# Start of a graph-network layer: which queue issues the filter taps, x and the first filter stores

## The chip, the cores and the metric

The kernel runs on one core of a Trainium2 chip. A core has a matrix engine (TensorE, PE in the profile, with its weight loads shown as PEld), a vector engine (VectorE, DVE), a scalar engine (ScalarE, ACT), GpSimd (POOL) and SyncE (SP), each with an instruction queue of its own, and 16 DMA engines that move data between HBM and the on-chip memory. SP, ACT and POOL issue transfers. The time is device microseconds of one execution; the figure for a kernel is the median of its runs.

## The reference, cut to what matters

Inputs are `x` (64 graphs, 256 nodes, 256 channels) and `adj` (64, 256, 256).

```
h  = relu(layernorm(x))
c  = relu(bn1(conv1x1(h)))
c  = bn2(conv17(c, w2, pad=8))                 # 17 taps, 256x256 channels
x_conv = relu(c + h)
s  = h @ w_se.T + b_se
A  = exp(-|s_i - s_j|^2) * adj
x_nmp = A @ relu(h @ w_msg.T + b_msg)
out = x + GRU(input=[x_conv, x_nmp], state=h)
```

## The kernel before

Graphs are handled in pairs; pair `i` is one tile `x` of 128 x 1024 elements, loaded by two transfers of 256 KB (`load_x`, `load_rows`, L377). Four pairs make a block, and eight blocks are run. The 17-tap convolution is done in a transformed domain: the sequence is cut into 16 phases, a hand-written transform (class `Fft`, on DVE) turns the activations into 16 frequency points, matrix products with transformed filters are made per point (`products`), and the transform is undone. The transformed filters are made once, at the start, and kept in HBM.

That start is what the change touches. The raw filter is read as `taps`: 128 input channels of each half `dc` in 19 groups of seven channels, so that a group fills 7 x 17 = 119 partitions. `load_taps(dc, a, b, eng)` (L451) loads groups a to b of one half in one transfer. A third has six groups, 119 x 6 rows of 1 KB, 714 KB. The nineteenth group is left over and comes by `load_last_taps` (L456), 34 KB for each half. `points` (L569) are three constant matrices with the roots for three sets of frequency points, called passes 0, 1 and 2.

`filters(m, g, eng)` makes group g for pass m: four matmuls in the trace, two for each half (L479), into an `acc` bank; one copy by ACT into `fo` (L646), of which there are six buffers; and one store of `fo` to the HBM tensors `filt` by the queue `eng` (L647). A copy into `fo` must wait until the store that used the same buffer six calls ago has landed. There are 57 such calls. The list `steps` begins with all three passes of groups 0 to 5, which need the first third of the taps alone, and goes on pass by pass with the other groups.

The first 16 calls are made among the work on the first block, in the loop over j from 0 to 3 (L877). A round j does: `transpose_h(j)` for j > 0 (PE transposes the normed x, ACT writes `hT` with a relu, L599, and at its end `load_x(j + 2)` is issued into the buffer that was just read), `norm(j + 1)` for j = 1 and 2 (DVE statistics L517 to L522, GpSimd's power L523 into `rstd`, DVE's scaling L526), `conv1(j)` (PE, then ACT into `h1`, L618), the first steps of the transform (DVE, L62 and L65) and four calls of `filters`. Round 0's `transpose_h(0)` and `norm(1)` stand ahead of the loop. In round 2 a set of small loads is issued too: nine on GpSimd (L890, L893, L467) and `w_msg` and the first `adj` on SP.

After the loop the other 41 calls of `filters` run, with stores on SP and GpSimd in turn, while DVE does the transform. When the stores of a pass have landed, `load_kind` (L658) reads the transformed filters back as `wb`. All later blocks follow.

The order on each engine is the order in which the code is written (`manual_schedule`). [...] In the kernel before SP issues, in this order: x0, x1; half 0, first third; x2; half 0, second third; four stores; x3; the last third of both halves and the two small loads; four stores; x4, `w_msg`, `adj`; four stores; x5; four stores; and then its share of the later stores. ACT issues half 1's first third, the points and half 1's second third.

## Time and profile before

| | |
|---|---|
| median of 5 runs | 1898.44 us (1896.26 to 1901.28) |
| profiled execution: time | 1899.55 us |
| profiled execution: span | 1897.8 us |
| PE busy in the span | 1836.1 us (97%) |
| DVE busy | 1398.1 us (74%) |
| ACT busy | 637.5 us (34%) |
| POOL busy | 206.4 us (11%) |
| mean granted TensorE clock | 0.989 |

Times in the profile are microseconds from the start of the span. A line of a timeline has the start, the length, the engine, the source line, the operation, output and inputs, and in square brackets the time that the engine was idle before it and what ended that wait. An SP or ACT line with a q is an issue of a transfer: it occupies the queue and not an arithmetic engine, and its length is how long the queue was held in it. Lines for the same group are merged (x4), and a merged length runs from the first start to the last end. A table by stretches of time gives busy microseconds of each engine, the clock granted to TensorE as a share of full speed, the mean busy share of the 16 DMA engines, and the rate.

### The profile page before, as it was taken

To read this page: it belongs to the slowest core of one execution; us is meant where nothing else is said; L and a number is where in the kernel's file an instruction comes from. 1 tells how busy PE (TensorE), PEld (TensorE's weight loads), DVE (VectorE), ACT (ScalarE), POOL (GpSimd) and SP (SyncE) were. 2 spreads that over 40 slices of the span, in tenths; PEclk is the share of its full clock that TensorE was granted. 3 is DMA by queue.
4 is the path that set the end of the run, shared out by engine and by line. 5 is a ranking of instruction groups with operands and counts; after the bars stand their busy time and mean duration, and the time that the engine had idled before them with its cause. 6 is when DMAs were issued, how large, how long until landed. Compare 5 with 4: busy or idle time off the path is not lost.

```text
span 1897.8 us, 21985 instructions
## 1 busy us (share of the span) xinstructions
PE 1836.1 (97%) x7710; PEld 1140.2 (60%) x7710; DVE 1398.1 (74%) x2675; ACT 637.5 (34%) x1335; POOL 206.4 (11%) x324
## 2 busy tenths in 40 slices
PE   6899999999999999999999999999999999999997
PEld 3677445875549554694458755495546944586543
DVE  5777648996499945998389964999559983798522
ACT  2424322243313443244222433134432352324311
POOL 2110110100111010111101001101101111010000
PEclk9889999999999999999999999999999999999999
DMA  5776331662328431482316613174314813063010
GB/s 177 251 245 198 93 80 35 193 178 56 85 49 243 108 93 52 115 235 56 89 34 194 178 55 84 52 239 111 89 55 111 240 56 78 23 190 99 1 44 22
DMA packets 179071, 217.63 MB, mean 115 GB/s; under 512 B 85038, under 2 KB 104778, under 8 KB 178961
## 3 DMA queue, kind: packets, MB, share of 16 engines
q1 hardware_dynamic: 146389, 157.61, 28.9%
q0 software_dynamic: 30464, 56.73, 12.2%
q10 hardware_dynamic: 2108, 1.89, 0.3%
q8 instruction: 61, 1.00, 0.2%
q14 instruction: 49, 0.40, 0.1%
HBM read 156.54 MB, written 44.30 MB: 106 GB/s over the span
## 4 chain that ended last, share of the span: by engine, by line
PE 82%; DVE 8%; issue 3%; DMA 3%; ACT 2%; POOL 1%; ACTq 0%; POOLq 0%; SPq 0%; DVEq 0%
PE acc L479 70%; PE aux L479 8%; PE aux L483 3%; DVE Yv L59 1%; PE aux L759 1%; DMA taps<-in_c_wT_dram 1%; DVE e L766 1%; DVE Yv L62 1%; DVE T L65 1%; DVE Yv L65 1%; DMA wb<-filt 1%; DMA x<-in_x_dram 1%; DVE msg L731 1%; DVE V L65 1%; DVE T L62 0%
## 5 line engine op out<-in xcount | busy, mean ns | idle before, releaser
L479 PE MATMUL acc<-hT,w_hh 128*128 128x512 f32 x768 | 355.6, 599 | 3.0 <-ACT h L618 3.0
L479 PE MATMUL acc<-xnm,w_ih 128*128 128x512 f32 x768 | 352.8, 593 | 0.0
L479 PE MATMUL acc<-Yv,w_ih 128*128 128x512 f32 x768 | 341.1, 593 | 9.6 <-ACT Yv L719 9.6
L479 PEld LDWEIGHTS acc<-Yv,w_ih 128*128 128x128 f32 x768 | 145.1, 190 | 196.4 <-issue 177.2
L479 PEld LDWEIGHTS acc<-xnm,w_ih 128*128 128x128 f32 x768 | 145.6, 190 | 183.1 <-issue 181.1
L479 PEld LDWEIGHTS acc<-hT,w_hh 128*128 128x128 f32 x768 | 144.0, 192 | 171.9 <-issue 162.7
L820 ACT ACTIVATE tr<-acc,b_rz 128x512 f32<-128x512 f32 x64 | 44.0, 687 | 540.8 <-PE acc L479 540.8
L822 DVE SCALAR_TENSOR_TENSOR gn<-tr,gn 128x512 f32<-128x512 f32 x64 | 44.2, 691 | 208.5 <-ACT tr L820 208.5
L848 POOL DMA_DIRECT2D out_dram<-y x64 | 39.0, 615 | 889.0 <-DVE y L847 859.9
L479 PE MATMUL acc<-hT,w_c 128*128 128x512 f32 x256 | 120.6, 615 | 10.1 <-ACT hT L599 9.2
L479 PE MATMUL acc<-U,wb 128*128 128x128 f32 x1024 | 125.4, 277 | 1.4 <-DMA wb<-filt 1.4
L479 PE MATMUL acc<-V,wb 128*128 128x128 f32 x1024 | 124.8, 275 | 0.0
L479 PEld LDWEIGHTS acc<-U,wb 128*128 128x128 f32 x1024 | 121.3, 193 | 5.3 <-DVE Yv L59 2.3
L59 DVE SCALAR_TENSOR_TENSOR V<-T,V 128x256 f32<-128x256 f32 (+2 forms) x224 | 121.6, 609 | 0.3
L479 PEld LDWEIGHTS acc<-V,wb 128*128 128x128 f32 x1024 | 119.5, 192 | 0.0
L479 PE MATMUL aux<-e,msg 128*128 128x256 f32 x464 | 104.9, 379 | 0.0
L479 PEld LDWEIGHTS aux<-e,msg 128*128 128x128 f32 x464 | 86.1, 190 | 11.4 <-issue 1.0
L847 DVE TENSOR_TENSOR y<-aux,y 128x512 f32<-128x512 f32 x64 | 41.1, 685 | 68.4 <-PE aux L483 68.4
L479 PE MATMUL aux<-w_msg,hT 128*128 128x259 f32 x384 | 90.8, 386 | 0.0
L523 POOL TENSOR_TENSOR rstd<-rstd,neg_half 128x4 f32<-128x4 f32 x32 | 36.3, 1133 | 497.8 <-DVE rstd L522 497.7
L479 PEld LDWEIGHTS acc<-hT,w_c 128*128 128x128 f32 x256 | 50.1, 197 | 61.6 <-issue 47.6
L65 DVE TENSOR_TENSOR V<-h 128x512 f32<-128x512 f32 x64 | 43.8, 685 | 53.2 <-ACT h L618 53.2
(148 smaller groups left out, 2734.4 us busy)
## 6 DMA issues: line engine op xcount, KB each, us to landing
wb<-filt SPq DMA_DIRECT2D x376, 256.0 KB
x<-in_x_dram SPq DMA_DIRECT2D x64, 256.0 KB
y<-in_x_dram POOLq DMA_DIRECT2D x64, 256.0 KB, 5.4
out_dram<-y POOLq DMA_DIRECT2D x64, 256.0 KB, 5.2
halves_d<-halves SPq DMA_DIRECT2D x116, 128.0 KB
adjh<-halves_d POOLq DMA_DIRECT2D x116, 128.0 KB, 5.3
filt<-fo SPq DMA_DIRECT2D x24, 252.0 KB
filt<-fo POOLq DMA_DIRECT2D x12, 252.0 KB, 5.0
```

The source lines that it names most:

```text
L59: return self.step(out, lambda: self.v.scalar_tensor_tensor(out, x, s, y, op0=ALU.mult, op1=ALU.add))
L62: return self.step(out, lambda: self.v.tensor_add(out, x, y))
L65: return self.step(out, lambda: self.v.tensor_sub(out, x, y))
L479: nc.tensor.matmul(p, w, v, **kw)
L483: nc.tensor.transpose(p, v, ident)
L523: nc.gpsimd.tensor_tensor(t["rstd"], t["rstd"], neg_half, ALU.pow)
L731: nc.vector.tensor_add(MSG[i][:, g, c, :], p[:, :D + SE], b_msg)
L759: nc.tensor.matmul(p[:, :N], ZT[rows_q, :P], ZT[rows_q, P:], start=True, stop=True)
L820: nc.scalar.activation(tr, pr, AF.Tanh, bias=b_rz[:, dc:dc + 1], scale=0.5)
L822: nc.vector.scalar_tensor_tensor(gn, tr, 1.0, gn, op0=ALU.add, op1=ALU.mult)
L847: nc.vector.tensor_add(row_tile(Y[i], g), p, row_tile(Y[i], g))
L848: nc.gpsimd.dma_start(out=rows(out, G * i + g), in_=row_tile(Y[i], g))
```

## The change

The first, second and last third of half 0 are issued on SP right behind x0 and x1, and the last third of half 1 and the two small loads behind `transpose_h(0)`. x2 and x3 are issued on GpSimd's queue, behind the memsets at the start and behind the stores of round 0. The stores of rounds 0, 1 and 2, twelve in all, are issued on GpSimd's queue; those of round 3 stay on SP. ACT's own issues and the order on PE, DVE and ACT stay as they are. In the changed file lines up to 470 keep their numbers, lines 476 to 874 are higher by one, and lines from 888 on are lower by two.

```diff
-    load_taps(0, *THIRDS[0], nc.sync)
+    for t in THIRDS:
+        load_taps(0, *t, nc.sync)
     load_taps(1, *THIRDS[0], nc.scalar)
...
         if i + 2 < B // G:
-            load_x(i + 2)
+            load_x(i + 2, nc.gpsimd if i < 2 else nc.sync)
...
     transpose_h(0)
-    load_taps(0, *THIRDS[1], nc.sync)
+    load_taps(1, *THIRDS[2], nc.sync)
+    for dc in range(DC):
+        load_last_taps(dc, nc.sync)
     norm(1)
     for j in range(PB):
         if j > 0:
             transpose_h(j)
-        if j == 1:
-            for dc in range(DC):
-                load_taps(dc, *THIRDS[2], nc.sync)
-            for dc in range(DC):
-                load_last_taps(dc, nc.sync)
...
         for m, n in steps[j * 4:(j + 1) * 4]:
-            filters(m, n, nc.sync)
+            filters(m, n, nc.gpsimd if j < 3 else nc.sync)
```

## The prediction

> **What bounds the kernel now.** I read the share table first: PE is busy 97% of the span, so a saving counts only where PE itself waits. Then I read the granted clock in 2 us slices, which drops to half in one early place, and then the timelines of PE, ACT and SP around it. PE's timeline, 19 to 64 us (start, length, group, and in brackets the idle time before it and its cause):

> ```profile
> 21.98 1.10 PE L479 MATMUL acc<-taps,points 119*126 119x256 f32 x4 [2.52 <-DMA points<-points]
> 23.65 2.86 PE L479 MATMUL acc<-taps,points 119*126 119x256 f32 x12 [0.58 <-DMA points<-points]
> ...
> 36.19 3.70 PE L479 MATMUL acc<-hT,w_c 128*128 128x512 f32 x8 [0.47 <-ACT hT L599]
> 39.72 3.62 PE L479 MATMUL acc<-taps,points 119*77 119x256 f32 x16
> 43.18 1.04 PE L483 MATMUL aux<-ident,x 128*128 128x128 f32 x8
> 52.63 6.76 PE L479 MATMUL acc<-hT,w_c 128*128 128x512 f32 x8 [8.42 <-ACT hT L599]
> ```

> PE works almost without a gap from 22 to 44 us, then stands for 8.42 us. The same eight matmuls of conv1 take 3.70 us at 36.19 and 6.76 us after the stall. It waits for ACT's hT, so next is ACT's timeline, and SP's queue below it:

> ```profile
> 41.65 0.59 ACT L646 COPY fo<-acc 126x512 f32<-126x512 f32 x1 [0.28 <-PE acc L479]
> 50.95 1.14 ACT L646 COPY fo<-acc 126x512 f32<-126x512 f32 x2 [8.71 <-DMA filt<-fo]
> 51.99 1.08 ACT L599 ACTIVATE hT<-aux 128x512 f32<-128x512 f32 x2
> ```

> ```profile
> 23.73 3.74 SPq L647 DMA_DIRECT2D filt<-fo  x4
> 27.57 6.18 SPq L377 DMA_DIRECT2D x<-in_x_dram  x2
> 33.80 3.66 SPq L451 DMA_DIRECT2D taps<-in_c_wT_dram  x2
> 37.50 6.11 SPq L456 DMA_DIRECT2D taps<-in_c_wT_dram  x2
> 43.70 1.94 SPq L647 DMA_DIRECT2D filt<-fo  x4
> ```

> The hT copy stands in ACT's queue behind two copies into fo, and these wait 8.71 us for an earlier store out of fo, because fo has six buffers. The second four stores' data were ready at 32.9 to 35.6 us (ACT's copies at 32.29 to 34.33), but SP only issued them from 43.70 on: from 27.57 to 43.6 us it was held in the loads of x3 and of the taps' last third. The semaphore records in the trace have the first of these stores land at 50.8 us, just before ACT goes on at 50.95. So the cause is the order of SP's queue. The clock shows the second half of the loss (us, PE, PEld, DVE, ACT, POOL, granted clock, DMA share, GB/s):

> ```profile
> 22.00:24.00 2.00, 1.42 (x6) 0.94 (x7) 2.00 (x5) 0.58 (x1) 0.00 (x0) 1.00 0.47 162
> ...
> 46.00:48.00 2.00, 0.00 (x0) 0.00 (x0) 0.00 (x0) 0.00 (x0) 0.60 (x2) 1.00 0.85 280
> 48.00:50.00 2.00, 0.00 (x0) 0.00 (x0) 0.00 (x0) 0.00 (x0) 0.00 (x0) 0.64 0.62 208
> 52.00:54.00 2.00, 1.37 (x2) 0.84 (x3) 0.00 (x0) 1.06 (x3) 0.00 (x0) 0.50 0.73 234
> ```

> **Part 1, stores of j = 0 to 2 leave SP.** The four stores of j = 1 then go out on POOL when their data is there, about 33 to 36 us, and the wait goes. In the rounds before, PE stands 0.30 and 0.47 us between the x transposes and conv1. Conv1 of j = 3 can start at 43.18 + 1.04 + 0.47 = 44.7 instead of 52.63: 7.9 us. From conv1's start to the filter matmuls it is 59.23 - 52.63 = 6.60 us after the stall and 39.72 - 36.19 = 3.53 us without it: 3.1 us for the clock. Sum 11.0 us.

> **Part 2, what POOL takes on.** 12 stores (0.53 us each, the median of POOL's rows for L647) and 4 x issues (0.61 us each, the POOL rows of L377): 6.4 + 2.4 = 8.8 us on an engine that is busy 12.5 of the first 64 us. What is queued behind them is rstd (L523), 1.01 us each, which norm needs. POOL's new order is x2, rstd(1), four stores, x3, rstd(2), four stores, rstd(3), nine small loads of j = 2, four stores.
> - rstd(1): x2 is issued after the memset of h ends (14.06) and takes until about 15.3; DVE has the input at 16.06. Nothing.
> - rstd(2): x3 needs the transposes of x1 (until 27.4), is issued until 28.7; rstd(2) ends near 29.8 instead of 26.7, and DVE's scale (1.38) near 31.2. The transposes of x2 start at 34.68: hidden with 3.5 us to spare.
> - rstd(3): the stores of j = 1 end near 36.2. POOL's loads of y, the nearest rows, land after 4.6 to 9.6 us, median 6.4, so x3 lands at 34 to 38 instead of 39.2. The transposes of x3 are due at 43.18, and DVE's statistics, rstd and scale take 1.5 + 0.4 + 0.2 + 1.1 + 1.5 = 4.7 us: hidden by 0.5 to 4 us.
> - The four stores of j = 2 stand behind the nine small loads (5.6 us of issue; the last has to wait until the first has landed, 5.3 us after its issue). They start near 45 instead of 51.57, ahead of before, and with 5.0 us to land free fo at about 50 to 52; ACT needs that at about 51. Between nothing and 1 us; I take nothing, as PE has five accumulators in hand.

> **Part 3, all taps at once.** SP loses 16 issues and issues its four large and two small tap loads back to back. Only the first thirds are needed before 64 us. Between 8 and 24 us taps and points come at 147 to 177 GB/s with the DMA share at 0.47 to 0.53, in every slice: these loads keep about half of the engines full and the others empty. So more taps in SP's queue add no speed, and they are queued behind the first third, which costs it nothing. What is new is x2 beside both first thirds, where it came after them: 512 KB over all engines, of which a share of 0.45, some 230 KB, falls on the half that taps use, at their 160 GB/s: 1.4 us. In return the points, which shared with x2, get through sooner. The first filter matmul slips by 0 to 1.4 us; I take 0.7, on PE's path. If all taps took equal turns with the ACT queue, nothing more is lost, since SP's queue is still one queue. The last taps land near 47 us by the bytes, 48.6 before; they are needed about 59 us. Behind the taps on SP now stand x4, w_msg, the first adj, x5 and the stores of j = 3. [...]

> After j = 3 the filter stage is paced by its own stores (ACT waits for "DMA filt" 12 times between 74 and 100 us, DMA share 0.8 to 1.0), by wb, and DVE's transform, all of which start from the work of j = 3 and move with it. I see nothing up to 110 us that is tied to absolute time, and from there on PE is busy. The gain stays: 11.0 - 0.7 = 10.3 us.

> [...] In the trace PE idle from 19.46 to 21.98 (2.5 us) kept it; 44.2 on lost it at 48.6 and had it back at 58.9. With 0.7 to 1.4 us more the early gap reaches 3.2 to 3.9 us. [...] By the row, no drop. I take no drop, as the likelier, and keep the other as a rival.

> **Time.** The profiled execution took 1899.55 us, span 1897.8 and 1.75 around it; less 10.3 it is 1889.2. It lay 1.1 over the median of the runs, so 1898.44 - 10.3 = 1888.1.

> **Rivals.**
> - A, the above, 0.66: 1888.1, own range 1884 to 1892. The low end is a second half-clock stretch, at 100 to 110 us, that also goes.
> - B, half of it lost, 0.18: the drop above, or fo late by 1 to 2 us at several places. 1893, and in one case in six over 1894.6.
> - C, the change does not do what it says, 0.07: the stall is moved, as POOL's last four stores, behind the nine small loads, hold ACT at j = 3. Against it is the start near 45. It needs 10 us more. 1898.
> - D, slower, 0.09: POOL's stores land late, because they share engines with two queues full of taps. The seventh copy needs the first store (ready 24.4, needed 35.0: 10.6 us), the eleventh the fifth (9.7), the fifteenth the ninth (about 6). With a landing of L us, (L - 10.6) + (L - 9.7) + (L - 6) reaches 10.3 at L = 12.2. With L = 15 the stalls add up to 18.7, giving 1898.4 + 8.4 = 1907. For it: SP's first store, queued behind taps, took 10.5 us (23.73 to 34.2). Against it: POOL's stores take 2.5 to 6.6, and small POOL loads amid the last taps 5.3.

> **Numbers.** 0.2% (3.8 us) is about what a measurement of this kernel tells from no change. Faster: A and five sixths of B, 0.66 + 0.15 = 0.81. Same: 0.03 + C = 0.10. Slower: D, 0.09. The range 1883 to 1895 takes in A but for a little, and B; C, D and odd ends of A stay outside, about 0.2.

> **What would show it.** PE's row for conv1 of j = 3 near 45.5 us, 3.7 us long; no wait of ACT for "DMA filt" before 60; SP's tap loads all issued ahead of any store; rstd(2) later, with no PE wait for x; filter stage over near 97. Wrong if the first filter matmul comes after 24 us or at half clock, if ACT waits for a filt store at the seventh, eleventh or fifteenth copy, or if PE's later idle time grows by what is saved here.

## The result, and the profile after

The changed kernel takes 1893.06 us (median of 43 runs, 1887.48 to 1897.18) against 1896.44 us for the kernel before (80 runs): a ratio of 0.998, 95% interval 0.9975 to 0.9985. By the ratio that is 3.8 us, 2.8 to 4.7 (the two medians alone differ by 3.4). Faster, as forecast, but with little more than a third of the 10.3 us. The profiled execution took 1890.98 us, its span is 1889.0 us.

PE's timeline of the changed kernel, in the columns explained above:

```profile
23.36 5.19 PE L480 MATMUL acc<-taps,points 119*126 119x256 f32 x16 [4.98 <-DMA points<-points]
28.38 1.04 PE L484 MATMUL aux<-ident,x 128*128 128x128 f32 x8
...
45.09 1.04 PE L484 MATMUL aux<-ident,x 128*128 128x128 f32 x8
46.46 3.70 PE L480 MATMUL acc<-hT,w_c 128*128 128x512 f32 x8 [0.34 <-ACT hT L600]
50.00 3.62 PE L480 MATMUL acc<-taps,points 119*126 119x256 f32 x16
...
62.63 3.81 PE L480 MATMUL acc<-taps,points 119*126 119x256 f32 x11 [2.60 <-ACT fo L647]
```

The stall ahead of conv1 of round 3 is gone: 0.34 us of waiting where 8.42 us stood, and conv1 takes 3.70 us instead of 6.76. Round 3's filter matmuls start at 50.00 instead of 59.23 us. But PE now waits in two other places: 4.98 us (2.52 before) for the points ahead of the first filter matmul, and 2.60 us at 60.0 behind ACT's `fo`. The first of them also halves the clock (table by stretches: us, PE, PEld, DVE, ACT, POOL, granted clock, DMA share, GB/s):

```profile
22.00:24.00 2.00, 0.65 (x2) 0.59 (x3) 2.00 (x6) 0.00 (x0) 0.00 (x0) 0.75 0.49 160
24.00:26.00 2.00, 2.00 (x6) 1.59 (x5) 0.77 (x6) 0.56 (x1) 0.00 (x0) 0.50 0.48 168
```

ACT's timeline shows what PE waits for at 60.0:

```profile
55.03 0.58 ACT L647 COPY fo<-acc 77x512 f32<-77x512 f32 x1 [2.52 <-DMA filt<-fo]
56.04 0.58 ACT L647 COPY fo<-acc 126x512 f32<-126x512 f32 x1 [0.42 <-DMA filt<-fo]
56.98 1.31 ACT L647 COPY fo<-acc 126x512 f32<-126x512 f32 x2 [0.35 <-DMA filt<-fo]
61.99 1.83 ACT L647 COPY fo<-acc 126x512 f32<-126x512 f32 x3 [3.71 <-DMA filt<-fo]
```

And SP's queue shows which stores those are:

```profile
4.77 25.12 SPq L451 DMA_DIRECT2D taps<-in_c_wT_dram  x4
29.93 11.30 SPq L456 DMA_DIRECT2D taps<-in_c_wT_dram  x2
41.66 1.62 SPq L377 DMA_DIRECT2D x<-in_x_dram  x2
43.34 0.74 SPq L893 DMA_DIRECT2D w_msg<-in_msg_wT_dram  x1
44.13 5.98 SPq L377 DMA_DIRECT2D adj<-in_adj_dram  x2
50.28 1.24 SPq L377 DMA_DIRECT2D x<-in_x_dram  x2
51.68 31.33 SPq L648 DMA_DIRECT2D filt<-fo  x17
```

SP is through with the taps at 41.2 us and then issues x4, `w_msg`, `adj` and x5, 1.75 MB, until 51.5 us, held 5.98 us in `adj` alone. The first store of round 3 goes out at 51.68, right behind its copy, so SP costs it nothing at the issue. But it is last in a queue of loads: by the semaphore records it has landed at 61.9, after 10.2 us, and ACT's copy at 61.99 is the one that needs its buffer. In the kernel before the same store was issued at 60.9 and landed at 65.1, after 4.2 us.

The same records show the wait in parts. A store of 126 partitions is counted up in 14 landings. Of this one six come from 55.3 to 56.3 us and eight from 58.7 to 61.9, the last right behind the last load ahead of it (the second half of x5, 61.2). A load of x or `adj` on SP is counted in 8 landings and a large tap load in 7, where `w_msg` has 16. That fits a store of which about half the parts stand behind these loads on the same engines; which engines they are is not on record.

In sum, ACT's waits for filter stores (us, times, longest) after round 3 are 22.7 us, between 50 and 106:

```profile
ACT fo L647 <- DMA filt<-fo: 22.7, 17, 3.7
```

and were 14.0 us in the like stretch before, from 59 to 111:

```profile
ACT fo L646 <- DMA filt<-fo: 14.0, 11, 2.4
```

The first message product (`w_msg`, PE's first work behind the filter stage) starts at 102.04 instead of 107.12 us, first before, then after:

```profile
107.12 4.30 PE L479 MATMUL aux<-w_msg,hT 128*128 128x259 f32 x12
```

```profile
102.04 4.29 PE L480 MATMUL aux<-w_msg,hT 128*128 128x259 f32 x12
```

So of the 9.2 us at round 3's first filter matmul, 5.1 are left there. The spans differ by 8.8 us; the other 3.7 come later, where the order of work is the same, and the medians don't have them. In this pair they go with the clock: between the first message product and PE's last matmul of the GRU it stood at half for 16.5 us before and 9.7 after, which is worth about 3.4 us (an estimate: half of the difference).

### The profile page after: what moved, and what is told of

It reads as the page before. It is cut to its first block, busy times and chain, and to the rows that moved or that the text cites. A ratio compares the mean times of both kernels' runs of the same rounds, so it can differ in the third digit from the quotient of the medians.

```text
span 1889.0 us, 21985 instructions
## 1 busy us (share of the span) xinstructions
PE 1831.7 (97%) x7710; PEld 1139.8 (60%) x7710; DVE 1398.0 (74%) x2675; ACT 637.1 (34%) x1335; POOL 215.3 (11%) x340
## 3 DMA queue, kind: packets, MB, share of 16 engines
q1 hardware_dynamic: 144373, 153.87, 28.7%
## 4 chain that ended last, share of the span: by engine, by line
PE 82%; DVE 8%; issue 3%; DMA 3%; ACT 2%; POOL 1%; POOLq 0%; ACTq 0%; DVEq 0%
PE acc L480 70%; PE aux L480 8%; PE aux L484 3%; DVE Yv L59 1%; PE aux L760 1%; DVE e L767 1%; DVE Yv L62 1%; DMA points<-points 1%; DVE T L65 1%; DVE Yv L65 1%; DMA x<-in_x_dram 1%; DMA wb<-filt 1%; POOL filt L648 1%; DVE msg L732 1%; DVE V L65 1%
## 5 line engine op out<-in xcount | busy, mean ns | idle before, releaser
L823 DVE SCALAR_TENSOR_TENSOR gn<-tr,gn 128x512 f32<-128x512 f32 x64 | 44.2, 691 | 208.9 <-ACT tr L821 208.9
L527 DVE TENSOR_SCALAR x<-x,mv,rstd 128x256 f32<-128x256 f32 x128 | 44.3, 409 | 50.6 <-POOL rstd L524 50.6
L480 PEld LDWEIGHTS aux<-w_msg,hT 128*128 128x128 f32 x384 | 72.6, 192 | 14.9 <-issue 4.7
```

The costliest lines, as they stand in the source:

```text
L480: nc.tensor.matmul(p, w, v, **kw)
L527: nc.vector.tensor_scalar(X[i][:, j, :], X[i][:, j, :], t["mv"][:, j, 0:1], t["rstd"][:, j:j + 1], ALU.subtract, ALU.mult)
L823: nc.vector.scalar_tensor_tensor(gn, tr, 1.0, gn, op0=ALU.add, op1=ALU.mult)
```

## The experiments

Every ratio is to the kernel before, run on the same chip. One ruler serves for all: the start of ACT's n-th copy into `fo`, read from the trace and counted from 0 (so are the twelfth and twentieth copy in the last expectations). Copy 0 shows when the filters begin; copy 12 is the first of round 3; copy 56 is the last. A row shows the one profiled execution, its last column the median of all runs. Undisturbed, the eight steps from copy 12 to copy 20 take 7.3 us.

```
                                     copy 0  copy 12  copy 20  copy 56  12 to 20  first message  median us
before                                 23.1     60.3     67.6    107.3      7.3       107.1       1896.4
before, second profile                 25.8     59.8     67.1    105.8      7.3       105.5       1895.8
changed                                25.4     51.1     63.2    102.2     12.2       102.0       1893.1
changed, second profile                26.6     53.4     65.0    103.1     11.6       102.8       1892.1
stores alone                           25.4     51.1     66.0    106.6     14.9       106.4       1895.7
taps and x alone                       26.4     67.7     75.0    113.3      7.3       113.2       1899.6
loads behind round 3's stores          25.7     51.8     59.1    103.2      7.3       103.0       1895.7
without the last third of the taps     26.5     53.3     60.6     99.3      7.3        98.9       1888.1
seven fo buffers                       26.5     52.8     63.5    100.8     10.7        97.2       1888.6
split tap loads                        20.7     49.5     56.8     95.5      7.3        94.9       1886.0
x4, x5, adj behind the stage           26.5     53.0     60.3     98.8      7.3        98.7       1897.5
x4, x5, adj still later                27.6     54.5     61.8     99.9      7.3        99.2       1888.9
other taps behind x2                   24.8     51.8     65.7    104.3     13.9       104.2       1893.6
```

The theories have letters in the expectations. Q: the order in the queues is what costs, and a better order wins the gain back. W, later E: the bytes that were moved during PE's stall still have to be moved, by DMA engines that the tap loads fill only in part (a DMA share of 0.48 from 8 to 14 us in the changed kernel). T: the early taps are the cause. B: six `fo` buffers and the time of a store set the pace of the filter stage. L: the stores of round 3 meet x4, x5, `w_msg` and `adj`.

### The two halves of the change, each alone

The kernel before with its stores of rounds 0 to 2 on GpSimd and nothing else:

```diff
-            filters(m, n, nc.sync)
+            filters(m, n, nc.gpsimd if j < 3 else nc.sync)
```

> The kernel before with one part of the change alone: the twelve stores of rounds 0 to 2 on GpSimd's queue; taps and x stay on SP as before. Theory Q (the gain comes from taking stores out from behind SP's loads; part of it is lost again because other stores stand behind loads): the 8.7 us wait of ACT before the eleventh copy goes, the first filter matmul comes at 22.0 as before, and the time is that of the changed kernel or up to 2 us less, 1891 to 1893. Theory T (the early taps are what brings the gain): 1896, no change from before. Theory W (the filter stage ends when the DMA engines are through with its bytes, whatever the order): as the changed kernel, PE's first message product near 102.

1895.66 us, ratio 0.9997 (0.9987 to 1.0007): nothing. PE's and ACT's rows show why:

```profile
46.46 3.70 PE L479 MATMUL acc<-hT,w_c 128*128 128x512 f32 x8 [0.34 <-ACT hT L599]
...
65.36 5.06 PE L479 MATMUL acc<-taps,points 119*126 119x256 f32 x11 [5.34 <-ACT fo L646]
```

```profile
64.72 1.83 ACT L646 COPY fo<-acc 126x512 f32<-126x512 f32 x3 [6.49 <-DMA filt<-fo]
```

The stall goes in full and comes back: PE waits 5.34 us at 60 us, because round 3's first store, issued at 54.4 behind x4, `w_msg`, `adj` and x5, lands at 64.6, after 10.2 us. Of the three expectations only T's number, 1896, came, and the next run speaks against T.

The changed kernel with its stores all on SP again, so that taps, x2 and x3 alone are changed:

```diff
-            filters(m, n, nc.gpsimd if j < 3 else nc.sync)
+            filters(m, n, nc.sync)
```

> The changed kernel with one part undone: all filter stores on SP again, so the taps come early and x2, x3 go out on GpSimd, but the stores stand behind every tap load. Order theory: SP is in tap loads until about 41 us, the first stores land near 48 to 50, ACT's seventh copy (due near 35) waits 12 us or more, PE stands as long and loses its clock; the transfers of x4, w_msg, adj drain meanwhile, so the filter stage that follows is as fast as in the kernel before (first message product 108 to 112), 1898 to 1904. Rival (the early taps are what brought the gain, the place of the stores is nothing): 1892 to 1894.

1899.60 us, ratio 1.0021 (1.001 to 1.0032): 4 us slower, as the order theory said. SP is in tap loads until 42.0 us, and ACT waits 11.64 us for the first store:

```profile
49.80 0.59 ACT L647 COPY fo<-acc 126x512 f32<-126x512 f32 x1 [11.64 <-DMA filt<-fo]
```

```profile
51.93 6.49 PE L480 MATMUL acc<-hT,w_c 128*128 128x512 f32 x8 [11.79 <-ACT hT L600]
```

After this longer stall the filter stage is undisturbed: copy 12 to 20 in 7.3 us, a first store of round 3 that lands after 2.5 us. Neither half gains; together they gain 3.8 us.

### The loads in the queues

x4, `w_msg`, `adj` and x5 behind round 3's stores on SP, that is behind the loop over j (the changed kernel otherwise):

```diff
-        if i + 2 < B // G:
+        if i + 2 < B // G and i not in (2, 3):
             load_x(i + 2, nc.gpsimd if i < 2 else nc.sync)
...
-            nc.sync.dma_start(out=w_msg[:, :, :D], in_=msg_wT.rearrange("(k p) o -> p k o", p=P))
-            load_adj(0, nc.sync)
...
+    nc.sync.dma_start(out=w_msg[:, :, :D], in_=msg_wT.rearrange("(k p) o -> p k o", p=P))
+    load_adj(0, nc.sync)
+    load_x(4)
+    load_x(5)
```

> The changed kernel, with x4, x5, w_msg and the first adj issued on SP behind the stores of round 3 instead of ahead of them. Theory Q: the stores of copies 13 and 14 land near 57 instead of 61; ACT's 3.7 us wait before copy 19 goes, PE's 2.6 us gap at 60 too; the first message product comes near 99 instead of 102, and the time is near 1890. Theory W: the wait moves to later copies, the message product stays at 101 to 102, and the time at 1893.

1895.69 us, ratio 0.9993 (0.9983 to 1.0003). Theory Q (1890) falls; W has the place of the waits right, but not the time (1893). Round 3's first store now lands after 2.9 us, and copy 20 comes at 59.1; but the waits stand eight copies later:

```profile
63.07 0.59 ACT L647 COPY fo<-acc 126x512 f32<-126x512 f32 x1 [2.51 <-DMA filt<-fo]
65.47 0.59 ACT L647 COPY fo<-acc 126x512 f32<-126x512 f32 x1 [1.82 <-DMA filt<-fo]
67.04 0.59 ACT L647 COPY fo<-acc 126x512 f32<-126x512 f32 x1 [0.98 <-DMA filt<-fo]
```

From copy 20 to 28 it takes 13.9 us where the kernel before takes 7.0. The loss follows the loads.

The nine small loads at the very start of GpSimd's queue, and no longer in round 2:

```diff
+    w_msg = const.tile([P, DC, D + SE], FP)
+    nc.gpsimd.dma_start(out=w_msg[:, :, D:], in_=se_wT.rearrange("(k p) s -> p k s", p=P))
+    b_msg = const.tile([P, D + SE], FP)
+    for t, v in ((b_msg[:, :D], msg_b), (b_msg[:, D:], se_b)):
+        nc.gpsimd.dma_start(out=t, in_=bass.AP(tensor=v.tensor, offset=v.offset, ap=[[0, P], [1, v.shape[0]]]))
+    load_vectors("bn2", bn2 + [ih_b, hh_b], nc.gpsimd)
     load_vectors("bn1", bn1, nc.scalar)
...
```

> The changed kernel, with the nine small loads of round 2 issued on GpSimd at the very start, so that the stores of round 2 have nothing of theirs ahead. Theory Q: these stores go out from 44 us on instead of 49 to 51, ACT's 2.5 us wait before copy 15 goes; as SP's stores of round 3 still come late, most of it is lost again before copy 19: message product at 101 to 102, time 1891.5 to 1893. Theory W: message product at 102, 1893.

1893.64 us, ratio 0.9983 (0.9975 to 0.9991): no different from the change itself. In its profiled execution, which took 1898.21 us, the first filter matmul comes at 25.57 us, later still, and copy 12 to 20 takes 12.6 us.

Both edits:

> Both edits: SP's four sets of loads behind the stores of round 3, and the nine small loads at the start. Theory Q: no wait of ACT for a filt store before 62 us, message product near 97 to 98, time 1888 to 1889.5. Theory W: message product at 101 to 102, time 1893, with ACT's waits for filt stores between 62 and 100 us larger by what is missing ahead of 62.

1897.67 us, ratio 1.0004 (0.9997 to 1.0011). As with the first edit alone, copy 12 to 20 takes 7.3 us and copy 20 to 28 14.1 us. Two repairs of order bring nothing; together they even cost the change's gain (W expected 1893), with the first message product at 106.4 us.

### Bytes and engines

The changed kernel without the last third of the taps (the two 714 KB loads are left out, the tile's part is filled with a constant, so the filters of groups 12 to 17 are not the reference's):

```diff
+    nc.gpsimd.memset(taps[:, THIRDS[2][0]:THIRDS[2][1]], 0.01)
-    for t in THIRDS:
+    for t in THIRDS[:2]:
         load_taps(0, *t, nc.sync)
...
-    load_taps(1, *THIRDS[2], nc.sync)
```

> The changed kernel without the loads of the last third of both halves (1.43 MB left out, the tile is filled with a constant instead, so the filters of groups 12 to 17 are not the reference's). Theory E: the engines have 9 us less of this load to do, ACT's waits before copies 15 and 19 go, message product at 95 to 98 instead of 102, time 1886 to 1889. Theory B (the stage is paced by six fo buffers and the time a store takes, whatever else is moved): first waits go, but the stage still takes 45 us or more from its start, message at 99 to 101, 1890 to 1892.

1888.1 us, ratio 0.9949 (0.9934 to 0.9965). Copy 12 to 20 takes 7.3 us and the stage doesn't pay it back later. With 1.4 MB less in the queues, round 3's first store lands after 4.1 us, though x4, `w_msg`, `adj` and x5 are still ahead of it. The time is theory E's; the first message product, 98.9, lies between E's 95 to 98 and B's 99 to 101.

Each large tap load as two transfers, of 112 and 7 partitions; all bytes stay:

```diff
-        eng.dma_start(out=taps[:, a:b, dc, :],
-                      in_=c2_wT[dc * P + a * KG:dc * P + b * KG].rearrange("(g k) t o -> (k t) g o", k=KG))
+        src = c2_wT[dc * P + a * KG:dc * P + b * KG].rearrange("(g k) t o -> (k t) g o", k=KG)
+        eng.dma_start(out=taps[:112, a:b, dc, :], in_=src[:112])
+        eng.dma_start(out=taps[112:, a:b, dc, :], in_=src[112:])
```

> The changed kernel, with each large tap load issued as two transfers, 112 partitions and 7, instead of one of 119. Theory E (tap loads fill only about half of the DMA engines, and what the kernel before moved while PE stood still has to be moved all the same, so that the wait comes back in the filter stage): with 112 rows all 16 engines work, DMA share between 10 and 20 us goes from 0.5 to 0.8 or more, the first filter matmul comes at 18 to 20 us instead of 23.4, no half clock there, ACT's waits ahead of 62 us shrink, the first message product comes at 93 to 97 instead of 102, time 1883 to 1888. Theory Q (order of queues alone): first filter matmul 1 to 2 us earlier, waits at copies 15 and 19 as before, message at 100, 1891.

1886.0 us, ratio 0.9938 (0.9922 to 0.9954). The table by stretches, first of this kernel, then of the changed one:

```profile
8.00:14.00 6.00, 3.14 (x9) 1.97 (x10) 3.81 (x15) 0.81 (x2) 3.77 (x7) 1.00 1.07 270
```

```profile
8.00:14.00 6.00, 3.06 (x9) 1.98 (x10) 3.82 (x15) 0.00 (x0) 3.69 (x7) 1.00 0.48 165
```

The DMA share goes from 0.48 to 1.07 and the rate from 165 to 270 GB/s. In the semaphore records a load of 112 partitions has 16 landings, one of 119 had 7. The first filter matmul starts at 19.6 us with no lost clock, copy 12 to 20 takes 7.3 us. All of it is as theory E expected.

The same split in the kernel before:

> The same two transfers in the kernel before, with its order of queues. Theory E: SP is through with its taps sooner, ACT's 8.7 us wait before the eleventh copy shrinks to 0 to 4 us, message product at 96 to 102 instead of 107, time 1886 to 1892; the change of queues is then worth 2 to 4 us on top. Theory Q: the wait stays at 6 us or more, 1894 to 1896.

1887.01 us, ratio 0.9943 (0.9929 to 0.9957). With quick taps the old order stalls PE far less:

```profile
42.45 3.70 PE L480 MATMUL acc<-hT,w_c 128*128 128x512 f32 x8 [1.94 <-ACT hT L600]
```

Then it meets the late loads too: copy 12 to 20 takes 11.7 us. Beside the split the change of queues is worth 1 us, with intervals that overlap, and not the 2 to 4 us that E expected.

Seven `fo` buffers in the changed kernel:

```diff
-        t = stage.tile([P, W], FP, name="fo", bufs=6)
+        t = stage.tile([P, W], FP, name="fo", bufs=7)
```

> The changed kernel with seven fo buffers instead of six (as many as fit). Theory B: the filter stage takes about 6/7 of its 48 us, message product near 96, time 1887 to 1889. Theory E: each wait moves one copy later, message product at 100 to 102, 1891 to 1893.

1888.57 us, ratio 0.9956 (0.9939 to 0.9973). The time is as theory B said, and so, nearly, is the first message product (B: 96):

```profile
97.17 4.54 PE L480 MATMUL aux<-w_msg,hT 128*128 128x259 f32 x12
```

From copy 20 to there it takes 33.6 us instead of 38.8 and 37.7, close to B's six sevenths. ACT's copies don't show it: from copy 20 to 56 they take 37.2 us instead of 39.0 and 38.1, and from 12 to 20 still 10.7. PE is now 3.6 us ahead of the last copy, where it was level with it before.

The same in the kernel before:

> The kernel before with seven fo buffers and no other edit. Theory B: the stall ahead of j = 3 stays (now the twelfth copy waits for the store of the fifth, and stands ahead of the same hT copy), conv1 of j = 3 at 52 to 53 us; the stage behind it goes from 43.7 to some 38 us, first message product 101 to 102, 1890 to 1891. So the gain of the seventh buffer is had without the change too, and the change is worth 2 to 3 us beside it. Rival (the buffers bind only in the changed kernel, where the stage meets the late loads): ACT's waits in the stage, 14.0 us before, are not all on PE's path, and the time is 1894 to 1896.

1891.37 us, ratio 0.9972 (0.9963 to 0.9981), near B's number, with the first message product at 101.96, where B had it. About 2 us of this lie ahead of copy 12, which comes at 58.1 us after a stall of 7.68 us; from copy 20 to the first message product it takes 36.0 us for 39.5 and 38.4. A buffer more helps either kernel by some 5 us; it doesn't explain the change.

Split and seven buffers together:

> The two edits that each gave some 5 to 8 us, together: every large tap load split into 112 and 7 partitions, and seven fo buffers. Theory B (from the stage after j = 3 on, the pace is the number of fo buffers over the time that a store takes; the split helps by starting the stage earlier and by leaving fewer bytes of taps in it): the two add, the stage from 54 to 94.9 us becomes 6/7 as long, first message product near 89 to 90, 1881. Theory E (the bytes still to be moved set the stage's end, and both edits only fill the DMA engines better): the second edit finds nothing left, first message product 94 to 95, 1885.5 to 1886.

1884.6 us, ratio 0.9936 (0.992 to 0.9952): within the interval of the split alone. So beside the split the seventh buffer brings no gain that these runs can tell. That is theory E's time, but the profile doesn't show E's reason: from copy 20 to the first message product it takes 34.9 us, 38.1 with the split alone, so the buffer does shorten the stage. What it wins there is lost ahead of it in this execution: copy 12 comes at 53.65, 49.48 with the split alone, after waits for the points and half clock from 25.8 to 32.7 us. B and E stay unseparated here. It is the fastest kernel here by its median, and both kernels with the split in the changed order beat the one before and the change.

### Second profiles

> The changed kernel once more, for a second profile: how much of its table is chance. If the give-back in the filter stage is its nature: first filter matmul within 1 us of 23.4, conv1 of j = 3 near 46.5 and 3.7 us long, first message product 101 to 104, ACT's waits for filt stores over 20 us between 50 and 106. If it was chance of one execution: a first message product near 97 to 98, with waits under 15 us. 1892 to 1894.

1892.08 us, ratio 0.998. All as the first expectation says, but two numbers: conv1 of round 3 is at 48.78, not 46.5, since the first filter matmul comes at 24.51. Copy 12 to 20 takes 11.6 us, the first message product is at 102.75. So what is lost again behind round 3 belongs to the kernel and not to one execution.

> The kernel before once more, for a second profile. If its table is its nature: first copy into fo 23 to 24, PE's stall ahead of j = 3 8 to 9 us, from the 12th to the 20th copy 7 to 8 us, first message product 106 to 108. If the first copy is at 25 and over, as in the kernel with the stores alone moved, the early slip of the changed kernel is at least in part chance. 1895 to 1898.

1895.81 us. This one taught most. PE, ACT and SP of the kernel before, second profile:

```profile
23.74 5.47 PE L479 MATMUL acc<-taps,points 119*126 119x256 f32 x16 [4.67 <-DMA points<-points]
...
52.58 6.31 PE L479 MATMUL acc<-hT,w_c 128*128 128x512 f32 x8 [5.79 <-ACT hT L599]
```

```profile
50.95 1.08 ACT L646 COPY fo<-acc 126x512 f32<-126x512 f32 x2 [6.14 <-DMA filt<-fo]
```

```profile
38.74 4.86 SPq L456 DMA_DIRECT2D taps<-in_c_wT_dram  x2
43.69 2.18 SPq L647 DMA_DIRECT2D filt<-fo  x4
```

PE starts its filters 1.76 us later than in the first profile and loses its clock there, as in the changed kernel. Yet SP comes out of the tap loads at 43.69 (43.70 in the first), ACT goes on at 50.95 (50.95), and conv1 of round 3 starts at 52.58 (52.63). Only the stall is shorter, 5.79 instead of 8.42 us. The stall is no fixed length; it ends at a gate at 50.95 us, and it swallows whatever PE loses ahead of it. What sets the gate is when SP is through with the taps: with the split tap loads in the same order SP was through with them at 31.75 instead of 43.6 us, and the stall was 1.94 us.

### Which loads, and what makes the start late

x4, x5 and the first `adj` (1.5 MB) behind the filter stage:

```diff
-        if i + 2 < B // G:
+        if i + 2 < B // G and i not in (2, 3):
...
-            load_adj(0, nc.sync)
...
         products(b, 0)
+        if b == 0:
+            load_adj(0, nc.sync)
...
         products(b, 2)
+        if b == 0:
+            load_x(4)
+            load_x(5)
```

> The changed kernel with adj of the first graphs, x4 and x5 (1.5 MB) loaded behind the filter stage instead of ahead of j = 3's stores; w_msg and the taps stay. Theory L (these loads are what the stores of j = 3 and after have to pass): the stretch from the 12th to the 20th copy into fo takes 7.3 to 8.5 us instead of 12, and later copies lose nothing in its place; first message product near 98 to 99, 1888 to 1889. Rival (it is the tail of the taps' last third, as the kernel without it suggests): the stretch keeps its 11 to 12 us, first message product near 102 to 103, 1892.

Within the stage theory L is right: copy 12 to 20 in 7.3 us, nothing paid back later, first message product at 98.65. But the kernel takes 1897.46 us, ratio 1.0008 (0.9997 to 1.0019), not 1888 to 1889. The loads now meet `w_hh` and `w_ih` on the way in, and PE waits for filters, with half clock from 135.0 us on for 10.24 us:

```profile
141.04 4.91 PE L480 MATMUL acc<-U,wb 128*128 128x128 f32 x24 [9.02 <-DMA wb<-filt]
```

The changed kernel waits 1.25 and 0.35 us there. So x4 and x5 were put past `w_hh` and `w_ih`:

```diff
         products(b, 2)
-        if b == 0:
-            load_x(4)
-            load_x(5)
...
         products(b, 4)
+        if b == 0:
+            load_x(4)
+            load_x(5)
```

> As the kernel with adj, x4 and x5 behind the filter stage, but x4 and x5 are issued behind the fifth group of products instead of the third, so that they don't meet w_hh and w_ih. Theory L: the stretch from the 12th to the 20th copy is 7.3 to 8.5 us and the first message product near 98.7 again, and the 9.0 us wait for wb falls to the 1 to 2 us that the changed kernel has there: 1888 to 1889.5, if x4 is still in time for its transposes near 157. If x4 comes late, PE waits for it there by some us: 1890 to 1894. Rival (the DMA engines are full up to 150 us, and what is taken out of the stage comes back later wherever it is put): 1892 to 1895.

1888.85 us, ratio 0.9959 (0.9944 to 0.9973). Copy 12 to 20 takes 7.3 us; the wait for `wb` is down to 0.98 us, and x4 is in time:

```profile
135.37 3.24 PE L480 MATMUL acc<-U,wb 128*128 128x128 f32 x24 [0.98 <-DMA wb<-filt]
```

That is 3.2 and 4.2 us under the two medians of the changed kernel: what was lost again is won back. It settles that the loss needs these loads, and that the rival (what is taken out of the stage comes back anywhere) is wrong. It needs the tap bytes too: without the last third, or with the taps split, the same loads stand ahead of round 3's stores and the stretch takes 7.3 us.

x2 on SP again behind the first third, with the other taps behind it as before the change:

```diff
-    for t in THIRDS:
-        load_taps(0, *t, nc.sync)
+    load_taps(0, *THIRDS[0], nc.sync)
...
-            load_x(i + 2, nc.gpsimd if i < 2 else nc.sync)
+            load_x(i + 2, nc.gpsimd if i == 1 else nc.sync)
...
-    load_taps(1, *THIRDS[2], nc.sync)
+    load_taps(0, *THIRDS[1], nc.sync)
+    for dc in range(DC):
+        load_taps(dc, *THIRDS[2], nc.sync)
```

> The changed kernel with x2 back on SP behind the first third of the taps, and the other taps behind x2, as before the change; x3 and the stores of j = 0 to 2 stay on GpSimd. If the taps queued ahead of x2 delay the start: first filter matmul 22.0 to 23.3, first copy near 23.1, twelfth copy near 49. Then either the two us stay (first message product 99.5 to 100.5, 1889 to 1890), or the stretch from the 12th to the 20th copy grows by as much, since the taps' last third still lands near 48 (first message product 101.5 to 103, 1891.5 to 1893.5); I hold the second likelier. If the start is not due to them: first filter matmul near 24.2, 1892.

1893.55 us, ratio 0.9988 (0.998 to 0.9997). The first filter matmul is at 23.66, inside the spread of the old order, and what the start gains the loads take: copy 12 to 20 in 13.9 us, first message product at 104.2. The second of the two answers was the nearer one; its 101.5 to 103 us for that product was still too early.

This edit with x4, x5 and `adj` behind the stage, and the split with the same:

> Both of the edits before together. Theory L with the early taps as cause of the late start: twelfth copy near 49, twentieth near 57, first message product 95.5 to 97.5, 1885.5 to 1887.5. If only one of them holds: 1888 to 1890. If neither: 1892.

> The changed kernel with the large tap loads split into 112 and 7 partitions, and adj, x4 and x5 behind the filter stage. The split alone already ran from the 12th to the 20th copy in 7.3 us, so by theory L nothing is left for the late loads to give there: first message product 94 to 95.5, 1885 to 1886.5, as with the split alone. Rival (every byte taken out of the stage shortens it): first message product 91 to 92, 1882 to 1883.

1898.23 us (ratio 1.001, 0.9999 to 1.0021) and 1898.51 us (1.0003, 0.9991 to 1.0015). Both times missed by 10 us and more. The profiles show what was seen above: waits of 10.35 and 9.38 us for `wb`, each with 10.24 us of half clock (the second's profiled execution took 1892.44 us, 6 us under its median, so not all of the miss is seen there). Inside the stage the two are as expected, or nearly: copy 12 to 20 in 7.3 us in both, first message product at 97.4 and 96.6 (95.5 to 97.5, and 94 to 95.5, were expected).

## Why the prediction was right or wrong

**The cause of the stall and its removal: right.** Stores behind the loads of x3 and the taps in SP's queue made it; taken off SP, they go out as forecast (L648 on GpSimd from 35.2 us), no copy waits up to round 2's end, and conv1 takes 3.70 us. `rstd` of x2 and x3 comes later, at 31.31 and 40.16, and no wait for x follows.

**The size of the stall: wrong in kind.** "Conv1 of j = 3 can start at 43.18 + 1.04 + 0.47 = 44.7 instead of 52.63" takes 8.42 us for a property of the kernel. It was the distance between a gate at 50.95 us and a start that happened to be early; the second profile has 5.79.

**"The first filter matmul slips by 0 to 1.4 us; I take 0.7": too little, and its setting was wrong.** In eight profiles with the new early order it comes at 23.4 to 25.5 us, mean 24.4; in six with the old order at 22.0 to 23.7, mean 22.9. The slip is 1.4, at the end of the range. The old kernel is late as well in some executions, and its gate hides that; the changed kernel has no gate, so each late start reaches the end of round 3.

**"By the row, no drop": wrong.** In all eight profiles of the new early order PE waits 4.28 to 6.03 us for the points, and each begins its filter matmuls at half clock; waits of 2.42 us (the kernel before with seven buffers) and 2.52 us (the kernel before) kept full clock. The row used was of one execution with an early landing. At what length an idle time of PE costs the clock was not shown, and the length of the wait alone doesn't decide it in these runs: waits of 2.82 us (stores alone) and 2.09 us (other taps behind x2, loads late) lost the clock as well. In these traces the granted clock changes only at steps of 3.41 us (up to 240 us its stretches at half last 3.41 or 10.24 us in the kernel before, 3.41 or 6.83 us in the changed one). In each of the 16 profiles (of 20) that lost it near the first filter matmul, PE was busy for 39% or less of one such step; the other four had no step there under 47%. The emptiest step of the four and the fullest of the sixteen (columns as in the table by stretches):

```profile
17.86:21.27 3.41, 1.60 (x4) 0.38 (x2) 3.31 (x8) 0.00 (x0) 0.00 (x0) 1.00 0.48 162
```

```profile
20.08:23.49 3.41, 1.32 (x5) 0.55 (x4) 2.73 (x6) 0.00 (x0) 0.00 (x0) 1.00 0.47 162
```

The first is of the kernel before, with PE busy for 1.60 us of 3.41; the second is of the other taps behind x2 with the loads late, with 1.32, and half clock from 23.49 on. So the kernel before was not far from losing it, and where the steps happen to lie decides too.

The three together, as copy 12 in the two pairs of profiles: 60.3 and 59.8 before, 51.1 and 53.4 after, 7.8 us instead of 10.3.

**The loads ahead of round 3's stores: the step that failed most.** The forecast takes nothing off the gain for them. SP was free in time to issue (51.5 us, the store goes at 51.68), but an issued store isn't a landed one: behind 1.75 MB in its queue it takes 10.2 us, where 4.2 and 5.0 were measured before. By copy 20 this costs 12.2 and 11.6 us for 7.3, so 4.6 us. The sentence that the full gain rests on, "I see nothing up to 110 us that is tied to absolute time", names the error: the tap bytes and the loads behind them are. (Its count of ACT's waits there is one too many, 11 and not 12, which changes nothing.) The kernel before let them pass while PE stood still. With 0.7 us won from copy 20 to the first message product, 7.8 - 4.6 + 0.7 = 3.9, against 3.8 by the ratio.

**Part 2's last four stores: nearly harmless.** They were to start near 45 us and started at 49.07: GpSimd came to the small loads at 41.16, and the last of them waited 2.28 us for the first to land. ACT's copy at 55.03 waits 2.52 us; PE works through, until the next wait.

**The rivals.** B, half of it lost by the early clock and by "`fo` late by 1 to 2 us at several places", is what came, with its 1893. The number is in part luck: B put half of the 10.3 us, about 5, on one of the two, and the runs have 2.5 us lost ahead of copy 12 and 4.6 us behind it. D is answered by the stores on GpSimd: 5.5 to 7.0 us to land, not 12, and no copy waits for one before copy 14 (55.03 us). C's stall is not there.

Not tried: round 3's stores on GpSimd as well. In the profile the first store that GpSimd issues after round 3, at 58.58, lands after 5.4 us amid the same transfers, so a part of the 10.2 us may be the place in SP's queue and not the load on the engines. The landings narrow this down, since six of the 14 parts of SP's store were in after 4.6 us behind the same issues, but the runs don't separate the two for the other eight. Whether the seventh buffer adds to the split is open too.

## What to carry to other kernels

A stall that ends at the same moment in every profile is a gate, not a duration: take a second profile before pricing it, find what sets the moment, and ask what else passes while the engine stands. When a wait is removed, follow the transfers that used its time, and price a store by when it lands behind what is queued ahead of it, not by when it can be issued. Before reordering queues, see whether the transfers fill the DMA engines.
